# Gated slot attention with a post-norm FFN on one core: ScalarE's copies of the gated transposes and the softmax's exponential change places, and some first transfers and weight sums are reordered

## The chip, the core and the metric

The kernel runs on one core of a Trainium2 chip. The metric is device time in microseconds. The engines are named as in the profile: PE is TensorE's matrix multiply, PEld its weight load, DVE is VectorE, ACT is ScalarE, POOL is GpSimd, SP is SyncE, which issues all transfers here.

## What is computed

The reference is a layer in two halves, each with a residual and a layer norm. The input `x` is 2 x 2048 x 512, all in float32. The heart of the first half, cut:

```python
q, k, v = heads(x @ Wq), heads(x @ Wk), heads(x @ Wv)      # 16 heads; 64, 64, 128
s = clip(heads(x @ Ws), -32, 32)                            # 64 slots
z = cumlogsumexp(s, time); g = exp(z_before - z); p = exp(s - z)
hk = hk * g + k (x) p ; ok = q . hk                         # per time step
pv = softmax(ok)                                            # over the 64 slots
hv = hv * g + p (x) v ; ov = pv . hv
o = rmsnorm(ov) * g_norm_weight * silu(x @ Wg)
x = layernorm(x + o @ Wo)
hidden = fwht(silu(x @ W1.T) * (x @ W3.T))                  # Walsh-Hadamard, 2048 wide
out = layernorm(x + hidden @ W2.T)
```

## The kernel before, in words

**Two phases.** The attention phase makes 64 steps: four groups of four heads (`g`), and for each group 16 chunks of 128 tokens (`n`), both batches side by side. It takes about the first 2430 us of the span. The FFN phase follows; the change does not touch it.

**Products in seven parts.** Every large product is a two by two block product with seven multiplications instead of eight (the Winograd form). So a step has products `q` (queries, keys and slot logits at once, L503), `v` (values and gates, L529) and `o` (the output projection, L746), each in seven parts 1 to 7, run in the order 1, 2, 5, 6, 7, 3, 4. The parts of one product are summed in three PSUM banks: parts 1, 6, 7, 4 in `c1` (two buffers), 5 and 3 in `c2`, 2 in `c3` (one buffer each; table `SUM`). After a part, VectorE or ScalarE reads the bank (`into`, L458 to L463, for `q` and `v`; L742 for `o`, which adds it to `rows`). `q`, `v` and `o` share the banks. So q2 needs `c3` free, that is, L742 must have read o2 from it; and o3 adds to the `c2` that L742 must have read for o5. Operands need block sums as well: for weights, `Weights.sums` (L408 to L414, four sums `k` = 0 to 3); for the left operand of `o`, `right_factor` (L425): ScalarE copies eight transposes from PSUM (L427, L428), VectorE makes two sums (L432, L433), GpSimd two more (L434, L435), the second from the first. The same `right_sums` serve the input tiles `xb` in the first group.

**Stages.** `run` (called with four steps: `new`, `now`, `before`, `old`) writes out by hand the order in which each engine gets its instructions; each engine's queue keeps that order. In one call step `now` does its `q` and `v` products, its scores and its softmax, while step `before`, one chunk earlier, gets its values, its gating, its transposes (`o_transposed`, L724) and o1, o5, o2; o3, o6, o7, o4 come in the next call, where the step is `old`. Only SP's order is made by the scheduler, from the same program.

**The place of the change in a step.** Part v7 is followed by `softmax` (VectorE: L625 product, L631 maximum, L633 difference; ScalarE: L634 exponential, in place on `r`), then v3, then `softmax_sum` (VectorE L638 sum and L639 reciprocal; GpSimd L640, `r` times `iz`), then `o_transposed` for step `before` (eight transposes L730 on TensorE into PSUM, then `right_factor` into `ob`), then `softmax_end` (VectorE L644, `r` times the reciprocal sum, after L640), then v4, tanh (L539), o1, o5, the gate product L543 and o2. The next call starts with q1, o3 and q2, with now and then a Hadamard product (L854) between o3 and q2, or transposes of finished rows (L905, L921) between o2 and q1. `r` is used next in that call, after q6 (L649).

**The start.** SP issues the input of step 0 (`load_x`: blocks 0 and 1 at L477, block 2 at L478, `b12` at L481), then four blocks of `wqks`, the fourth into the scratch tile `low` (L403), then the input of step 1, `wvg`, `wo_`. In the first step alone the four sums of `wvg` are in the list `late`: sum 0 before v1, sum 2 before v6, sum 1 before v5, sum 3 after v2. v6 needs sum 2, v7 needs sum 1, v3 needs sum 3. One tile `low` serves all weights, so `wo_`'s block into it waits for `wvg`'s sums.

Of the kernel before, what the change touches and what calls it, by code (L numbers as in the profile page):

```python
# [10 lines left out]
AF = mybir.ActivationFunctionType  # L11
# [8 lines left out]
DK = 64  # L20
# [18 lines left out]
def gated_slot_attention_ffn_kernel(  # L39
# [13 lines left out]
    nc = tc.nc  # L53
# [67 lines left out]
    wp = ctx.enter_context(tc.tile_pool(name="wp", bufs=1))  # L121
# [23 lines left out]
    def sums(pool, width, name):  # L145
        return {c: pool.tile([P, width], F32, name=name + c, tag=c, bufs=2 if c == "c1" else 1) for c in ("c1", "c2", "c3")}
# [3 lines left out]
    def open_x(name, outer, width):  # L150

        t = wp.tile([P, 7, 2, width], F32, name=name).rearrange("p a b c -> p (a b c)")
        for i, m in enumerate(outer):
            xb[RIGHT[m]] = t[:, i * 7 * TQ : (i + 1) * 7 * TQ].rearrange("p (k t) -> p k t", t=TQ)
            load_x(0, RIGHT[m])

    def open_acc(names, **where):
        t = where.pop("pool", hp).tile([P, len(names), 4, 2 * TQ], F32, name="acc" + names, bufs=1, **where)
        for i, n in enumerate(names):
            acc[n] = t[:, i]  # L160

    def load_x(blk, at):
        nc.sync.dma_start(out=xb[at], in_=fxd[blk][:, at])
# [46 lines left out]
    def up(u, h):  # L210
# [9 lines left out]
        for i, m in enumerate(OUTER):  # L220
# [13 lines left out]
            for k in INNER:  # L234
                s = c[SUM[k]]
                for j in range(2):
                    nc.tensor.matmul(  # L237
                        s[:, j * TQ : (j + 1) * TQ], lhsT=w[:, LEFT[k], j, :], rhs=right[:, RIGHT[k], :],
                        start=(k in (1, 2, 5) and j == 0), stop=True, skip_group_check=True,
                    )  # L240
                b = BLOCK[k]
                if k in (1, 5, 6, 4):
                    if first is None:
                        nc.scalar.copy(t[to][:, b], s)
                    else:
                        add(t[to], s, b, t[first])
                else:
                    add(t[to], s, b)
                if m in (6, 7) and k in ENDS:
                    o = t["w" if m == 6 else "v"][:, b]  # L250

                    (nc.gpsimd if u or m == 6 else nc.vector).tensor_tensor(o, o, t["u"][:, b], ALU.add)  # L252
                if k == 4:
                    if p == NSET - 1 and blk + 1 < NBLK:
                        load_x(blk + 1, RIGHT[m])
                    if m in (2, 6, 7, 4):
                        at, src = {2: (11, "x"), 6: (12, "w"), 7: (22, "v"), 4: (21, "u")}[m]
                        silu(h, at, t[src])
                yield
# [92 lines left out]
    with ExitStack() as att:  # L352
# [42 lines left out]
        class Weights:  # L395


            def __init__(self, name, blocks, pool=wp):
                width = blocks.shape[-1]
                self.t = pool.tile([P, 7, 2, width], F32, name=name)  # L400
                self.low = c1.tile([P, 2, width], F32, name="low", tag="low")
                for k, dst in enumerate((self.t[:, 0], self.t[:, 1], self.t[:, 2], self.low)):
                    nc.sync.dma_start(out=dst, in_=blocks[k])  # L403

            def sums(self, k, eng=nc.vector):
                t, low = self.t, self.low
# [6 lines left out]
                else:  # L413
                    eng.tensor_tensor(t[:, 6], t[:, 1], t[:, 4], ALU.subtract)  # L414

        def load_qks(g):
            return Weights("wqks", wqks[g])

        def load_vg(g):
            return Weights("wvg", wvg[g])  # L420

        def load_o(g):
            return Weights("wo_", wo[g], wpo)
# [41 lines left out]
        class Step:  # L465
# [4 lines left out]
            def load_x(self):  # L470
                self.xb = xp.tile([P, 7, 2, P], F32, name="xb")
                if self.g:
                    nc.sync.dma_start(out=self.xb, in_=xd[self.n])
                    return

                src = xt[self.n]
                nc.sync.dma_start(out=self.xb[:, 0:2].rearrange("p s c t -> p (s c) t"), in_=src[:, 0:KC])  # L477
                nc.sync.dma_start(out=self.xb[:, 2], in_=src[:, KC + 2 :])  # L478
                t = yp.tile([P, D], F32, name="b12", tag="rows")
                self.b12 = t[:, 0 : 2 * P].rearrange("p (c t) -> p c t", t=P)  # L480
                nc.sync.dma_start(out=self.b12, in_=src[:, KC : KC + 2])  # L481
# [140 lines left out]
            def softmax(self):  # L622

                self.r = r = c1.tile([P, NQ, 2 * M], F32, name="r", tag="r")
                nc.vector.tensor_tensor(  # L625
                    r.rearrange("p q (j m) -> p j q m", j=2), pn,
                    self.iz.rearrange("p q (j m) -> p j q m", j=2), ALU.mult,
                )
                self.r8 = r.rearrange("p q (j m) -> p (q j) m", j=2)
                mx = small.tile([P, 2 * NQ], F32, name="mx", bufs=2)  # L630
                nc.vector.tensor_reduce(mx, self.r8, AX.X, ALU.max)  # L631
                mxb = mx.rearrange("p (h o) -> p h o", o=1).to_broadcast([P, 2 * NQ, M])
                nc.vector.tensor_tensor(self.r8, self.r8, mxb, ALU.subtract)  # L633
                nc.scalar.activation(r, r, AF.Exp, scale=DK**-0.5)  # L634

            def softmax_sum(self):
                self.sm = small.tile([P, 2 * NQ], F32, name="sm")
                nc.vector.tensor_reduce(self.sm, self.r8, AX.X, ALU.add)  # L638
                nc.vector.reciprocal(self.sm, self.sm)  # L639
                nc.gpsimd.tensor_tensor(self.r, self.r, self.iz, ALU.mult)  # L640
# [354 lines left out]
        steps = [Step(g, n) for g in range(NG) for n in range(NCB)]  # L995
        w, nw = {}, {}

        def run(new, now, before, old):


            def do(step, name, *args):
                if step is not None:
                    getattr(step, name)(*args)

            def main(name, k):

                if now is not None:
                    getattr(now, name)(k)
                elif before is not None:
                    for _ in range(FILL[name, k]):  # L1010
                        next(ups)

            def work_on(place):

                if not changes:
                    y["place"] = place
                    next(pieces[0], None)
# [5 lines left out]
            def more():  # L1023

                if old is not None and old.g == NG - 1 and old.n >= NCB - 4:
                    work_on(1)
# [3 lines left out]
            g = now.g if now is not None else NG  # L1030
# [5 lines left out]
            late = [nw["vg"].sums] if now is steps[0] else []  # L1036
# [29 lines left out]
            if last:  # L1066
                nw["qks"] = load_qks(g + 1)
# [20 lines left out]
            do(before, "scores2")  # L1088
            do(now, "within1")
            do(before, "within2")  # L1090
            do(now, "share_of_keys")
            do(before, "share_of_values")
            do(now, "e_transposed")
# [9 lines left out]
            do(before, "gated")  # L1103

            for f in late:
                f(2)
            main("v", 6)
            more()
            for f in late:
                f(1)  # L1110
            main("v", 5)
            if o_last:
                scale_o()
            do(now, "reciprocal", 1)
            main("v", 2)
            more()
            for f in late:
                f(3)

            if last:  # L1120
                nw["qks"].sums(0, nc.gpsimd)
# [5 lines left out]
            do(now, "softmax")  # L1127
            main("v", 3)
            more()
            do(now, "softmax_sum")  # L1130
            if o_last:
                nw["o"].sums(2)
                nw["o"].sums(3, nc.gpsimd)
            do(before, "o_transposed")
            do(now, "softmax_end")
            main("v", 4)
            if last:
# [24 lines left out]
        with tc.manual_schedule(  # L1162
            engines={mybir.EngineType.PE, mybir.EngineType.DVE, mybir.EngineType.Activation, mybir.EngineType.Pool}
        ):
            steps[0].load_x()
            nw["qks"] = load_qks(0)
            steps[1].load_x()
            nw["vg"] = load_vg(0)
            nw["o"] = load_o(0)
            steps[0].make_x()  # L1170
            for k in range(4):
                nw["qks"].sums(k)
            N = len(steps)
            for i in range(N + 2):
                if i == N:
                    open_x("wvg", OUTER[3:], 4 * P)
                    open_acc("ux", tag="h1")
                    ups = up(0, h)
                run(*(steps[j] if 0 <= j < N else None for j in (i + 1, i, i - 1, i - 2)))
            for _ in pieces[0]:  # L1180
                pass
# [110 lines left out]
```

## Time and profile before

| | us |
|---|---|
| median of 3 runs | 3518.95 (3515.03 to 3519.06) |
| the profiled execution's own time | 3517.86 |
| its span, first to last instruction | 3516.1 |
| TensorE busy | 3456.7 |
| first matmul starts | 9.57 |
| length of an ordinary step in the first group | 36.74 |

The profile is of one execution, and its durations are that execution's. A row of a group gives line, engine, operation, tiles (out<-in, buffer numbers left out, so that `t` is `t1` or `t2`, `c` any of the banks), shapes and count, then busy time and the mean of one in ns, then the idle time of the engine before it and what ended that. A row of the timeline gives start, duration, engine, line, operation, tiles, shapes, count, and in brackets the idle time before it and its releaser. A matmul in float32 shows as two passes, so one part of `o` is a row of 4 matmuls. Ends of matmuls are modelled, and spans on GpSimd are rough. The weight loads (PEld) run ahead of the matmuls, so a wait often shows at the load first.

TensorE's granted clock is 1.00 in nearly the whole span.

### The profile page before, as it was taken

The page shows a single profiled execution, that of the slowest core. Times are in us where ns is not written, and L with a number is a line of the kernel's source. Part 1 is how long each engine was busy: PE and PEld are TensorE (multiplying, and loading weights), DVE is VectorE, ACT ScalarE, POOL GpSimd, SP SyncE. Part 2 cuts the span into 40 slices and gives each one's busy share as a digit, 9 for nine tenths or more (in the row PEclk, how much of TensorE's full clock was granted, in tenths as well). Part 3 has the DMA queues.
Part 4 walks back from the last instruction along what each step waited for, and adds up shares of the span by engine and source line. Part 5 has one row for each costly group of instructions (what it writes and reads, how often), then busy time and mean ns, then how long its engine had stood idle before and what let it go on. Part 6 is the DMA issues. An engine that isn't in the chain of part 4 may idle for free. (4 is left out here: it accounts for less than half of the span.)

```text
span 3516.1 us, 75258 instructions
## 1 busy us (share of the span) xinstructions
PE 3456.7 (98%) x31840; PEld 2702.8 (77%) x31840; DVE 2354.9 (67%) x3940; ACT 957.0 (27%) x1712; POOL 1144.2 (33%) x1069
## 2 busy tenths in 40 slices
PE   8999999999999999999999999998999999999998
PEld 6777777677777677677777777776888888888887
DVE  5777776665666765656766677777666756756756
ACT  3333333333333333333333333332111111111110
POOL 1222223221221331221332222223634643643544
PEclk9999999999999999999999999999999999999999
DMA  5334334221122232122222243347555544445431
GB/s 184 118 113 138 118 119 152 93 72 62 55 66 70 94 96 65 52 66 70 74 99 68 69 140 129 102 160 270 171 179 205 174 161 176 156 151 184 163 135 68
DMA packets 208833, 425.03 MB, mean 121 GB/s; under 512 B 19696, under 2 KB 120432, under 8 KB 207472
## 3 DMA queue, kind: packets, MB, share of 16 engines
q1 hardware_dynamic: 208496, 420.22, 35.7%
q8 instruction: 250, 4.10, 0.5%
q14 instruction: 87, 0.71, 0.1%
HBM read 297.47 MB, written 125.30 MB: 120 GB/s over the span
## 5 line engine op out<-in xcount | busy, mean ns | idle before, releaser
L529 PE MATMUL c<-wvg,xb 128*128 128x512 f32 x1792 | 812.7, 598 | 4.0 <-DVE wvg L412 2.0
L529 PEld LDWEIGHTS c<-wvg,xb 128*128 128x128 f32 x1792 | 322.1, 190 | 369.6 <-issue 291.9
L503 PE MATMUL c<-xb,wqks 128*128 128x128 f32 x3584 | 553.2, 277 | 15.7 <-DMA wqks<-wqks_blocks 9.6
L503 PEld LDWEIGHTS c<-xb,wqks 128*128 128x128 f32 x3584 | 479.9, 193 | 43.7 <-DVE rows L742 21.5
L218 DVE TENSOR_TENSOR accux<-c,accux 128x512 f32<-128x512 f32 x496 | 341.4, 691 | 180.9 <-PE c L237 163.5
L276 PE MATMUL dc<-w2t,hid 128*128 128x256 f32 x1792 | 455.3, 379 | 2.1 <-DVE res L283 2.1
L237 PE MATMUL c<-wvg,xb 128*128 128x256 f32 x1792 | 432.0, 380 | 6.1 <-DVE accux L218 5.3
L742 DVE TENSOR_TENSOR rows<-c,rows 128x256 f32<-128x256 f32 x448 | 181.7, 418 | 335.9 <-PE c L746 331.4
L237 PEld LDWEIGHTS c<-wvg,xb 128*128 128x128 f32 x1792 | 338.8, 190 | 56.9 <-DVE accux L218 9.1
L276 PEld LDWEIGHTS dc<-w2t,hid 128*128 128x128 f32 x1792 | 340.2, 190 | 49.5 <-DVE res L283 3.3
L503 PE MATMUL c<-wqks,xb 128*128 128x128 f32 x1792 | 347.4, 276 | 0.0
L463 DVE TENSOR_TENSOR t<-c,kept 128x384 f32<-128x384 f32 (+1 forms) x384 | 230.6, 611 | 155.6 <-PE c L503 147.5
L237 PE MATMUL c<-wqks,xb 128*128 128x256 f32 x1344 | 325.1, 380 | 5.2 <-DVE accux L218 2.3
L458 ACT COPY kept<-c 128x384 f32<-128x384 f32 (+1 forms) x384 | 203.5, 530 | 457.8 <-PE c L503 369.5
L516 POOL TENSOR_TENSOR e<-e,zc 1x512 f32<-1x512 f32 x60 | 76.4, 1273 | 710.0 <-ACT e L515 710.0
L237 PEld LDWEIGHTS c<-wqks,xb 128*128 128x128 f32 x1344 | 253.9, 190 | 44.0 <-DVE accux L218 5.0
L503 PEld LDWEIGHTS c<-wqks,xb 128*128 128x128 f32 x1792 | 273.0, 193 | 0.0
L283 DVE TENSOR_TENSOR res<-dc,res 128x256 f32<-128x256 f32 x448 | 189.2, 423 | 117.9 <-PE dc L276 107.3
L573 DVE RECIPROCAL iz<-z 128x256 f32<-128x256 f32 x128 | 223.9, 1749 | 44.6 <-ACT z L564 44.6
L710 POOL TENSOR_SCALAR ss<-ss 128x8 f32<-128x8 f32 x64 | 12.7, 198 | 685.3 <-DVE ss L708 685.3
L706 DVE TENSOR_TENSOR t<-po,t 64x512 f32<-64x512 f32 (+1 forms) x192 | 131.6, 685 | 95.6 <-ACT sq L704 94.3
L252 POOL TENSOR_TENSOR accw<-accw,accux 128x512 f32<-128x512 f32 x64 | 80.8, 1276 | 275.7 <-DVE accux L218 274.3
(189 smaller groups left out, 4975.7 us busy)
## 6 DMA issues: line engine op xcount, KB each, us to landing
xb<-w13s SPq DMA_DIRECT2D x112, 896.0 KB
xb<-xd SPq DMA_DIRECT2D x48, 896.0 KB
yd<-rows SPq DMA_DIRECT2D x128, 256.0 KB
w2t<-w2s SPq DMA_DIRECT2D x32, 896.0 KB
rows<-yd SPq DMA_DIRECT2D x100, 256.0 KB
xd<-xb SPq DMA_DIRECT2D x16, 896.0 KB
wvg<-fxd SPq DMA_DIRECT2D x16, 896.0 KB
w13s<-inner SPq DMA_DIRECT2D x96, 128.0 KB
```

The source lines that it names most:

```text
L218: nc.vector.tensor_tensor(into[:, b], s, (into if first is None else first)[:, b], ALU.add)
L237: nc.tensor.matmul(s[:, j * TQ : (j + 1) * TQ], lhsT=w[:, LEFT[k], j, :], rhs=right[:, RIGHT[k], :], start=(k in (1, 2, 5) and j == 0), st ...
L252: (nc.gpsimd if u or m == 6 else nc.vector).tensor_tensor(o, o, t["u"][:, b], ALU.add)
L276: nc.tensor.matmul(s, lhsT=h["hid"][:, i, LEFT[m], k * P : (k + 1) * P], rhs=h["w2"][:, i, RIGHT[m], :], start=(m in (1, 2, 5) and i == 0) ...
L283: nc.vector.tensor_tensor(r, s, r, ALU.add)
L458: nc.scalar.copy(self.kept[k], s)
L463: nc.vector.tensor_tensor(t[:, to], s, self.kept[other], ALU.add)
L503: nc.tensor.matmul(out[:, i * P : (i + 1) * P], lhsT=a, rhs=b, start=(k in OPENS and c == 0 and i == 0), stop=(c == 1), skip_group_check=True,
L529: nc.tensor.matmul(out, lhsT=self.xb[:, RIGHT[k], c, :], rhs=w["vg"].t[:, LEFT[k], c, :], start=(k in OPENS and c == 0), stop=(c == 1), sk ...
L573: nc.vector.reciprocal(self.iz[:, h], self.z[:, h])
L706: nc.vector.tensor_tensor(self.gj[to, j], self.po[j][at], self.gj[to, j], ALU.mult)
L742: nc.vector.tensor_tensor(y_, self.uo.sum(k), y_, ALU.add)
```

## The change

Three edits. First, the exponential L634 moves from `softmax` to the head of `softmax_sum`, and `o_transposed` of step `before` moves ahead of `softmax_sum`. So ScalarE's queue has L427, L428 and then the exponential; VectorE's has L432, L433 and then L638, L639; GpSimd's has L434, L435 and then L640. L644 still follows all of them on VectorE. TensorE's order stays as it was. In the steps that sum `wo_` (one in each of three groups), the sums k = 2, 3 stay behind `softmax_sum`.

Second, in the first step the late sums of `wvg` move up: sum 2 from before v6 to just behind `within2` (on VectorE between L584 and L602), sum 1 from before v5 to before v6, sum 3 from behind v2 to before v5 (ahead of the second half of L573).

Third, the first `load_x` issues only blocks 0 and 1 of `xb`; block 2 and `b12` (`load_rest`) follow behind the second block of `wqks`. SP's order changes with it at a few later places: in the first two steps the block of `wo_` into `low` moves ahead of half of a `zc` transfer and a `b12`, blocks 0 to 2 of step 2's input move ahead of three stores of `w13s`, and the store of `xd` for step 2 ahead of some more of those; near the end of the attention phase three transfers of the finished rows and of the FFN's tiles change places.

```diff
-            def __init__(self, name, blocks, pool=wp):
+            def __init__(self, name, blocks, pool=wp, then=None):
...
                 for k, dst in enumerate((self.t[:, 0], self.t[:, 1], self.t[:, 2], self.low)):
                     nc.sync.dma_start(out=dst, in_=blocks[k])
+                    if k == 1 and then is not None:
+                        then()
...
                 nc.sync.dma_start(out=self.xb[:, 0:2].rearrange("p s c t -> p (s c) t"), in_=src[:, 0:KC])
+                if self.n:
+                    self.load_rest()
+
+            def load_rest(self):
+                src = xt[self.n]
                 nc.sync.dma_start(out=self.xb[:, 2], in_=src[:, KC + 2 :])
...
-                nc.scalar.activation(r, r, AF.Exp, scale=DK**-0.5)
 
             def softmax_sum(self):
+                nc.scalar.activation(self.r, self.r, AF.Exp, scale=DK**-0.5)
                 self.sm = small.tile([P, 2 * NQ], F32, name="sm")
...
             do(before, "within2")
+            for f in late:
+                f(2)
             do(now, "share_of_keys")
...
             for f in late:
-                f(2)
+                f(1)
             main("v", 6)
             more()
             for f in late:
-                f(1)
+                f(3)
             main("v", 5)
...
             main("v", 2)
             more()
-            for f in late:
-                f(3)
...
             main("v", 3)
             more()
+            do(before, "o_transposed")
             do(now, "softmax_sum")
             if o_last:
                 nw["o"].sums(2)
                 nw["o"].sums(3, nc.gpsimd)
-            do(before, "o_transposed")
             do(now, "softmax_end")
...
-            nw["qks"] = load_qks(0)
+            nw["qks"] = load_qks(0, steps[0].load_rest)
```

## The prediction

> **What bounds the kernel now.** I read the page first, then TensorE's waits, then the timelines of one ordinary step and of the two places that the change touches elsewhere.
>
> From the page:
>
> ```profile
> PE 3456.7 (98%) x31840; PEld 2702.8 (77%) x31840; DVE 2354.9 (67%) x3940; ACT 957.0 (27%) x1712; POOL 1144.2 (33%) x1069
> L503 PEld LDWEIGHTS c<-xb,wqks 128*128 128x128 f32 x3584 | 479.9, 193 | 43.7 <-DVE rows L742 21.5
> ```
>
> TensorE bounds it: some 60 us of the 3516.1 are idle, so little can be won, while any new TensorE wait adds in full. The second row names a wait that exists already: weight loads of product q2 wait for L742. The list of who waits for whom (total us, times, longest), TensorE's matmuls, then its weight loads:
>
> ```profile
> PE c L503 <- DMA wqks<-wqks_blocks: 9.6, 1, 9.6
> ...
> PE c L746 <- ACT ob L427: 5.0, 8, 1.3
> ...
> PE c L529 <- DVE wvg L412: 2.0, 1, 2.0
> ```
>
> ```profile
> PEld c L746 <- ACT ob L427: 47.8, 64, 2.1
> ...
> PEld c L503 <- DVE rows L742: 21.5, 43, 1.6
> ```
>
> The first three lines are what the change aims at. The last matters most: in 43 of the 63 steps that hold both a softmax and an output product, q2 (bank c3) starts only when L742 has read product o2 from c3. The ordinary step, whose last transpose ends at 74.07:
>
> ```profile
> 73.65 0.69 DVE L633 TENSOR_TENSOR r<-r,mx 128x512 f32<-128x512 f32 x1
> ...
> 74.44 0.63 ACT L634 ACTIVATE r<-r 128x512 f32<-128x512 f32 x1 [5.82 <-DVE r L633]
> ...
> 74.98 0.57 ACT L427 COPY ob<-ps 128x512 f32<-128x512 f32 x1
> ...
> 75.94 1.28 POOL L640 TENSOR_TENSOR r<-r,iz 128x512 f32<-128x512 f32 x1 [3.01 <-PE c L529]
> ...
> 77.25 1.20 DVE L644 TENSOR_TENSOR r<-r,sm 128x512 f32<-128x512 f32 x1 [0.59 <-POOL r L640]
> 77.98 1.06 POOL L435 TENSOR_TENSOR ob<-ob 128x256 f32<-128x256 f32 x1
> ...
> 79.04 1.21 DVE L543 SCALAR_TENSOR_TENSOR t<-th,t 128x1024 f32<-128x1024 f32 x1
> ...
> 80.17 0.95 DVE L742 TENSOR_TENSOR rows<-c,rows 128x256 f32<-128x256 f32 x2
> 80.63 0.52 PEld L503 LDWEIGHTS c<-xb,wqks 128*128 128x128 f32 x4 [0.38 <-DVE rows L742]
> ```
>
> The chain is L640 on GpSimd, then on VectorE L644, L742 twice (o1, o5; from 78.37), L543, L742 for o2 (done 80.58), then q2's load at 80.63. There is no slack in it: what makes L644's end later makes TensorE later.
>
> **The change: the softmax's place, 63 steps.** Instructions stay the same, and TensorE's order does too. ScalarE has both `ob` copies ahead of the exponential; VectorE has L432, L433 ahead of L638, L639; GpSimd has L434, L435 ahead of L640. All three queues run in order. The last step has no softmax and shows the new order alone; its transposes end at 2431.52:
>
> ```profile
> 2431.60 0.59 ACT L427 COPY ob<-ps 128x512 f32<-128x512 f32 x1 [7.88 <-issue]
> 2432.09 0.38 ACT L428 COPY ob<-ps 128x256 f32<-128x256 f32 x1
> ...
> 2432.50 0.43 DVE L432 TENSOR_TENSOR ob<-ps,ob 128x256 f32<-128x256 f32 x1 [1.69 <-ACT ob L428]
> ...
> 2433.00 0.73 POOL L434 TENSOR_TENSOR ob<-ob 128x256 f32<-128x256 f32 x1 [2.63 <-DVE ob L432]
> ...
> 2433.81 0.72 POOL L435 TENSOR_TENSOR ob<-ob 128x256 f32<-128x256 f32 x1
> ```
>
> Laid on the step at 74.07: L427 at 74.15, L428 to 75.02, exponential (its input is ready at 74.34) 75.0 to 75.6, 0.55 later than now. VectorE: L432 75.05 to 75.47, L433 to 75.8, L638 to 76.41, L639 to 76.65. GpSimd: L434 75.55 to 76.28, L435 76.36 to 77.08. Only then L640, 77.05 to 78.33, though its input was there at 76.65. L644 starts at 78.36 instead of 77.25, 1.11 later.
>
> How long L644 then takes is one choice. It takes 1.20 beside L434 and L435, but 0.69 in the first step, where GpSimd stands idle after L640:
>
> ```profile
> 46.09 0.69 DVE L644 TENSOR_TENSOR r<-r,sm 128x512 f32<-128x512 f32 x1 [1.22 <-POOL r L640]
> ```
>
> In the new order nothing follows L640 on GpSimd, so I take 0.69: L644 ends at 79.05 against 78.45. The other choice is L435: 1.06 in ordinary steps, 0.72 alone. The Trainium skill (SBUF — State Buffer, "Who interferes with whom") says that a VectorE instruction with two SBUF inputs contends with a GpSimd one that reads SBUF, and that one with a single SBUF input, or a reduction, does not. L435 would now lie beside L638 and L639, both of the free kind: by the rule 0.72, shift 0.60; by the row of ordinary steps 1.06, shift 0.94. GpSimd's sum L408 of `wo_` (128x512), beside the reduction L631, takes 1.28 like L640 of the same shape: I take 0.60.
>
> Cost by step. 35 ordinary steps have q2's first matmul within 0.06 of o2's L742: 35 x 0.60 = 21.0. At three group ends GpSimd sums `wqks` until 2.84 after the transposes; L434, L435, L640 in a row then end at 5.65 against 4.08, L644 shrinks by 0.5: 3 x 1.07 = 3.2. In three steps that sum `wo_`, about 0.8 each, 2.4; in the last two softmax steps 0.7 each, 1.4. In twelve steps of the last group TensorE transposes rows (L905) between o2 and q1, and q2 starts 0.79 after L742: free. In eight steps L854 lies between o3 and q2 (0.77): q2 is free, o3 waits for o5's L742 some 0.1: 0.8. Sum 28.8 us. The ScalarE waits that go (5.0 at matmuls, some 0.1 hidden in the other loads) give nothing in the 43 steps: q2's wait is next and grows by what they shrink. `r` itself has time: its transposes (L649) come 8 us after L644. Tanh and v4's copy keep their times, as ScalarE is free from 75.6.
>
> **The change: the start.** The first matmul waits for `wqks` block 0, issued at 3.05 behind three `xb` transfers; two of them now go behind block 1, so it is issued 0.95 earlier, with 262 KB less ahead. q1 would start at 7.5 to 8.6 instead of 9.57. But q5 needs `low`, whose place is unchanged: L408 ended at 13.37, and q5 began at 14.82. So at most 1.4 is won, at least 0; I take 1.2. `wvg`'s issues slip by up to 2 us; its first use is at 22.68 and its sums start at 23.73.
>
> **The change: the first step's weight sums.** L412 now comes before L602 and the reciprocal L573, L414 before the second L573.
>
> ```profile
> 31.57 8.83 PE L529 MATMUL c<-wvg,xb 128*128 128x512 f32 x16 [1.96 <-DVE wvg L412]
> ...
> 32.55:35.97 3.42, 3.42 (x6) 1.36 (x5) 1.76 (x2) 0.59 (x1) 0.00 (x0) 0.50 0.69 184
> ```
>
> L412 takes 1.16 and would end at 27.6; L602 ends 28.0, before ScalarE's settle copy at 28.88 lets L617 go. The 1.96 goes, and 0.29 at v3. The second line is from the busy times by stretch (TensorE, loads, VectorE, ScalarE, GpSimd, then the granted clock): 0.50 granted for 3.42 us after a stretch (29.14 to 32.55) with TensorE busy 1.45 of 3.41. The Trainium skill (TensorE: Matmul & The Clock Gate, Part 1) has half clock follow at least one idle window; by its letter that window was not idle, and nothing would be won. By the row the gap brought it: 3.42 x 0.5 = 1.7 won. I side with the row. `low` of `wo_` is issued some 1 us sooner; half of zc, `b12` and the `w13s` stores behind moved entries on SP slip by a few us, each with tens of us to its use. Sum: 1.2 + 1.96 + 0.29 + 1.7 = 5.2 won.
>
> **Sum.** 28.8 - 5.2 = +23.6 on the profiled execution's own 3517.86: 3541.5. That execution lies 1.1 below the median of 3518.95, within the runs' spread; I say 3541.
>
> **Rivals.**
> - Not slower (10%): GpSimd's spans are rough, and L434 with L435 may hold it far less than 1.5 us. It decides once both take under 1.1 (75.55 to 76.65): then L640 starts as soon as L639 ends, L644 ends 0.1 later than now, and the waits for L427 are gone: -5.2 - 5.0 + 43 x 0.1 = 3512. For: loads wait for L427 in all 64 steps, 0.75 each. Against: L434 and L435 stand 0.08 apart at 0.73 and 0.72, and L644 starts 0.03 after L640's end, so that those spans fit their neighbours.
> - Half of it (8%): L742's wait grows by only 0.1 to 0.3 (L432 starts on L427 alone, shorter gaps): about 43 x 0.2 = +9, less 5.2, 3522.
> - Larger (12%): L435 at 1.06, shift 0.94: 35 x 0.94 + 8, and 0.2 in the free steps, less 5.2: 3558; with L644 still at 1.20 beyond that.
> - The start does nothing because the transfers share the engines anyway: 3542, inside the main case.
>
> **Numbers.** Main case 70%: 3530 to 3552. The range, to both sides, 3520 to 3558. A measurement can tell 0.2%, about 7 us, from no change: slower 0.83, same 0.11, faster 0.06.
>
> **What would show it.** Right: L640 ends near 4.3 after the transposes (now 3.15), L644 lasts 0.69, q2's load waits for L742 with more than twice the 21.5 us, L746's waits for L427 nearly vanish, ordinary steps are 37.3 us apart instead of 36.74; no half clock near 32. Wrong: step length unchanged in the first group, or L640 starting before L435 ends.

## The result, and the profile after

The changed kernel takes 3549.91 us (median of 5 runs, 3547.49 to 3555.39) against 3518.71 before: ratio 1.0095, 95% interval 1.0081 to 1.0109, 31 us slower where 22 were forecast. The whole interval lies above 1, so the loss is clear of noise. The profiled execution is the slowest of the five, 3555.39 with a span of 3553.6; sums below are made against its span, 37.5 above that of before (3516.1).

Behind the edited place the changed file counts lines higher: L408 is L410, L427 L429, L428 L430, L432 L434, L434 L436, L435 L437, L503 L510, L529 L536, L543 L550, L634 L643, L638 L645, L639 L646, L640 L647, L644 L651, L742 L749, L746 L753. Rows have the numbers of their own run's file. From the page after:

```profile
PE 3476.5 (98%) x31840; PEld 2727.2 (77%) x31840; DVE 2321.1 (65%) x3940; ACT 959.3 (27%) x1712; POOL 1120.2 (32%) x1069
L510 PEld LDWEIGHTS c<-xb,wqks 128*128 128x128 f32 x3584 | 487.9, 196 | 57.6 <-DVE rows L749 41.3
```

VectorE's busy time fell by 34 and GpSimd's by 24, although they execute the same instructions: in the ordinary step L644 takes 0.69 instead of 1.20, and L435 0.73 instead of 1.06, as they no longer run beside each other. That bought nothing, because the bound is TensorE's wait at q2, which nearly doubled (21.5 to 41.3 at the loads). The list of TensorE's waits, at matmuls and then at loads:

```profile
PE c L510 <- DVE rows L749: 19.7, 41, 3.8
PE c L753 <- DVE rows L749: 12.5, 11, 1.9
...
PE c L510 <- DMA wqks<-wqks_blocks: 6.4, 1, 6.4
```

```profile
PEld c L510 <- DVE rows L749: 41.3, 62, 4.2
...
PEld c L753 <- DVE rows L749: 18.2, 49, 1.6
PEld c L753 <- ACT ob L430: 14.4, 60, 0.2
```

The wait for the first copy (5.0 at matmuls, 47.8 at loads before) is gone; a short one for the second copy is left at the loads. In its place stand L749's, now at q2 in 62 steps instead of 43, and at o3 (L753) too. The same ordinary step as before, whose last transpose now ends at 66.79:

```profile
66.82 0.59 ACT L429 COPY ob<-ps 128x512 f32<-128x512 f32 x1 [5.49 <-PE ps L737]
...
67.57 0.65 ACT L643 ACTIVATE r<-r 128x512 f32<-128x512 f32 x1
67.72 0.42 DVE L434 TENSOR_TENSOR ob<-ps,ob 128x256 f32<-128x256 f32 x1
...
68.22 0.73 POOL L436 TENSOR_TENSOR ob<-ob 128x256 f32<-128x256 f32 x1 [2.58 <-DVE ob L434]
...
68.39 0.68 DVE L645 TENSOR_REDUCE sm<-r 128x8 f32<-128x512 f32 x1
...
69.03 0.73 POOL L437 TENSOR_TENSOR ob<-ob 128x256 f32<-128x256 f32 x1
69.10 0.20 DVE L646 RECIPROCAL sm<-sm 128x8 f32<-128x8 f32 x1
...
69.72 1.27 POOL L647 TENSOR_TENSOR r<-r,iz 128x512 f32<-128x512 f32 x1
...
71.02 0.69 DVE L651 TENSOR_TENSOR r<-r,sm 128x512 f32<-128x512 f32 x1 [1.72 <-POOL r L647]
...
73.42 0.75 DVE L749 TENSOR_TENSOR rows<-c,rows 128x256 f32<-128x256 f32 x2
73.90 0.52 PEld L510 LDWEIGHTS c<-xb,wqks 128*128 128x128 f32 x4 [0.74 <-DVE rows L749]
```

The first copy comes 0.88 sooner against the transposes. But GpSimd reaches L647 only after both its sums, VectorE then idles 1.72 in front of L651 (0.59 before) with the L749s queued behind it, and q2's load waits 0.74 instead of 0.38.

By kind of step, from the ends of the transposes in both traces:

| steps | change, us |
|---|---|
| start, to the first transposes | -7.3 |
| 35 ordinary | +19.7 (0.56 each) |
| 8 with L854 between o3 and q2 | +0.6 |
| 12 with L905 | -0.2 |
| 3 that sum `wqks` | +7.6 |
| 3 that sum `wo_` | +7.8 |
| last 2 with a softmax | +7.3 |
| after the last transposes | +1.9 |

The eight steps of the last three kinds are dearer than the mechanism's price. One of them, busy times by stretch (TensorE, loads, VectorE, ScalarE, GpSimd, then the granted clock, DMA share, GB/s):

```profile
596.00:599.42 3.42, 1.50 (x7) 1.05 (x8) 3.32 (x6) 0.00 (x0) 1.82 (x1) 1.00 1.02 418
599.42:602.83 3.41, 3.41 (x19) 3.41 (x18) 1.06 (x2) 0.00 (x0) 3.22 (x2) 0.50 0.63 263
```

Two waits for L749 (1.37 at o3, which begins before this stretch, and 1.21 at q2) leave TensorE busy 1.50 of 3.42, and in the next 3.41 the clock is granted by half. The profile after has eight such stretches in the eight steps, one of them of double length: with TensorE at work throughout 9 x 3.41 / 2 = 15.4 us, of 22.8. That is an upper estimate, and not all of it is the change's: the profile before has no half clock in the last two of these steps, but three other profiles with the old softmax order have it there (between 2394 and 2427), and in them these two steps are 0.8 to 3.4 us longer than in the profile before.

### The profile page after: what moved, and what is told of

Same layout as the page of the kernel before. It is cut to its first block, busy times and chain, and to the rows that moved or that the text cites. A ratio compares the mean times of both kernels' runs of the same rounds, so it can differ in the third digit from the quotient of the medians.

```text
span 3553.6 us, 75219 instructions
## 1 busy us (share of the span) xinstructions
PE 3476.5 (98%) x31840; PEld 2727.2 (77%) x31840; DVE 2321.1 (65%) x3940; ACT 959.3 (27%) x1712; POOL 1120.2 (32%) x1069
## 5 line engine op out<-in xcount | busy, mean ns | idle before, releaser
L536 PE MATMUL c<-wvg,xb 128*128 128x512 f32 x1792 | 810.7, 597 | 1.7 <-DVE t L465 0.9
L536 PEld LDWEIGHTS c<-wvg,xb 128*128 128x128 f32 x1792 | 321.6, 189 | 365.5 <-issue 289.6
L510 PE MATMUL c<-xb,wqks 128*128 128x128 f32 x3584 | 562.9, 280 | 27.1 <-DVE rows L749 19.7
L510 PEld LDWEIGHTS c<-xb,wqks 128*128 128x128 f32 x3584 | 487.9, 196 | 57.6 <-DVE rows L749 41.3
L749 DVE TENSOR_TENSOR rows<-c,rows 128x256 f32<-128x256 f32 x448 | 178.8, 420 | 330.7 <-PE c L753 330.6
L510 PE MATMUL c<-wqks,xb 128*128 128x128 f32 x1792 | 351.7, 279 | 0.0
L510 PEld LDWEIGHTS c<-wqks,xb 128*128 128x128 f32 x1792 | 277.7, 196 | 0.0
```

Source lines behind the costliest of these rows:

```text
L510: nc.tensor.matmul(out[:, i * P : (i + 1) * P], lhsT=a, rhs=b, start=(k in OPENS and c == 0 and i == 0), stop=(c == 1), skip_group_check=True,
L536: nc.tensor.matmul(out, lhsT=self.xb[:, RIGHT[k], c, :], rhs=w["vg"].t[:, LEFT[k], c, :], start=(k in OPENS and c == 0), stop=(c == 1), sk ...
L749: nc.vector.tensor_tensor(y_, self.uo.sum(k), y_, ALU.add)
```

## The experiments

My theory: L644 (here L651) is late, VectorE's queue carries that to L742 of o2, and bank c3 carries it to q2; three orders add up in it (exponential, VectorE, GpSimd); half clock follows where the waits get long. Rivals: the moved transfers; ScalarE's order alone; GpSimd's order alone. Each run below was timed beside the kernel before, whose median moves by some 3 us from one set of runs to the next, so differences are taken within a set.

**Start only.** The softmax as before, the other two edits kept:

```diff
+                nc.scalar.activation(r, r, AF.Exp, scale=DK**-0.5)
 
             def softmax_sum(self):
-                nc.scalar.activation(self.r, self.r, AF.Exp, scale=DK**-0.5)
...
-            do(before, "o_transposed")
             do(now, "softmax_sum")
...
+            do(before, "o_transposed")
             do(now, "softmax_end")
```

> Only the transfers and the first step's weight sums are reordered; the softmax's place is as before. Chain theory (the loss comes from L644 reaching q2's bank late): the ordinary step stays 36.74 us, the first step's gain of 7.3 us seen in the profile of the changed kernel stands alone: 3511 to 3512, no half clock near 32. If the start's gain were paid back later by the transfers that moved, 3518 to 3520.

Measured: 3510.14 against 3517.88, ratio 0.998 (0.9972 to 0.9987). The ordinary step is 36.74. The start's gain stands; the moved transfers cost nothing later.

**Softmax only.** The opposite: of the change only these lines.

```diff
-                nc.scalar.activation(r, r, AF.Exp, scale=DK**-0.5)
 
             def softmax_sum(self):
+                nc.scalar.activation(self.r, self.r, AF.Exp, scale=DK**-0.5)
...
+            do(before, "o_transposed")
             do(now, "softmax_sum")
...
-            do(before, "o_transposed")
             do(now, "softmax_end")
```

> Only the softmax's place is changed; the start is as before. Chain theory: ordinary step 37.31 us as in the changed kernel, 3550 + 7 = 3557. If part of the loss came from the moved transfers, less: 3545 to 3552.

Measured: 3556.67, ratio 1.0112 (1.0098 to 1.0126), ordinary step 37.30. The two halves add up: -7.7 and +38.8 give +31. The whole loss lies in the softmax's place.

**ScalarE's order only.** `right_factor` is split, so that the copies alone stand ahead of the exponential:

```diff
-                right_factor(self.ob, tp)
+                nc.scalar.copy(self.ob[:, 0:2].rearrange("p s c t -> p (s c) t"), tp[:, 0:4])
+                nc.scalar.copy(self.ob[:, 2], tp[:, 6:8])
+                self.tp12 = tp[:, 4:6]
+            def ob_sums(self, engines):
...
             do(now, "softmax_sum")
...
+            do(before, "ob_sums", "vp")
             do(now, "softmax_end")
```

> The changed kernel, but only ScalarE keeps the new order (both copies ahead of the exponential); VectorE has L638 and L639 ahead of its two ob sums and GpSimd has L640 ahead of its two, as before. Chain theory: the exponential ends at 1.47 after the transposes, L640 at 3.6, L644 3.64 to 4.84 (1.20, stretched again), 0.44 later than before: ordinary step 37.15, about 3518.7 - 7.3 + 43 x 0.4 = 3528. GpSimd's order as sole cause: 3512. ScalarE's order as sole cause: 3550.

Measured: 3533.26, ratio 1.0047 (1.0033 to 1.0061). The ordinary step is 37.17, as expected, and ScalarE's order as the sole cause (3550) falls. In this file L748 is the first of VectorE's two sums, L751 and L752 are GpSimd's, L764 is product `o`. The step whose transposes end at 178.66:

```profile
181.00 1.28 POOL L647 TENSOR_TENSOR r<-r,iz 128x512 f32<-128x512 f32 x1 [3.48 <-DVE sm L645]
181.01 0.39 DVE L748 TENSOR_TENSOR ob<-ps,ob 128x256 f32<-128x256 f32 x1
...
181.45 1.99 PE L764 MATMUL c<-wo__224,ob 128*128 128x256 f32 x8 [0.20 <-DVE ob L748]
...
182.31 1.20 DVE L651 TENSOR_TENSOR r<-r,sm 128x512 f32<-128x512 f32 x1 [0.59 <-POOL r L647]
183.03 1.06 POOL L752 TENSOR_TENSOR ob<-ob 128x256 f32<-128x256 f32 x1
```

L651 starts 3.65 after the transposes and lasts 1.20. So the copies' place costs 0.4 per step here, but by two routes that this run can't tell apart. Product o5 needs L748, which now stands behind L645 and L646, and waits for it, so that q1 starts some 0.4 later too. I had not counted that: the free steps, in which L644's lateness costs nothing, grow by as much (12 steps with L905: +4.8), and the total is 5 above what I expected. No half clock is granted in this execution before its end, and the eight special steps cost nothing (under 0.1 for each kind): there VectorE's L633 ends so late that the exponential starts no later than before, or nearly so.

**GpSimd's sums late.** The changed kernel with VectorE's sums where they are and GpSimd's behind L640: 

```diff
             do(before, "o_transposed")
+            do(before, "ob_sums", "v")
             do(now, "softmax_sum")
...
+            do(before, "ob_sums", "p")
             do(now, "softmax_end")
```

> The changed kernel, but GpSimd's two ob sums stand behind L640; ScalarE and VectorE keep the new order. Chain theory: L640 starts at 2.5 instead of 2.98 and ends at 3.8, but L644 is stretched to 1.20 again by the sums that now run beside it, and ends at 5.0 as in the changed kernel (4.97): ordinary step 37.3. In the three steps that sum wqks, L644 ends some 0.6 earlier, with fewer stretches at half clock: 3536 to 3545. GpSimd's order as sole cause: ordinary step 36.74, 3512.

Measured: 3544.6, ratio 1.0077 (1.0063 to 1.009), ordinary step 37.37. This refutes GpSimd's order as sole cause. In the step that ends its transposes at 179.32:

```profile
181.84 1.27 POOL L647 TENSOR_TENSOR r<-r,iz 128x512 f32<-128x512 f32 x1 [3.67 <-DVE sm L645]
183.08 0.73 POOL L751 TENSOR_TENSOR ob<-ob 128x256 f32<-128x256 f32 x1
183.15 1.20 DVE L651 TENSOR_TENSOR r<-r,sm 128x512 f32<-128x512 f32 x1 [1.21 <-POOL r L647]
```

L651 starts 0.4 sooner than in the changed kernel and takes 1.20 again instead of 0.69, as the sums run beside it. What GpSimd's order costs in waiting it gives back in that duration. The last two runs and the changed kernel differ from one to the next in one order, so the ordinary step can be split by engine: ScalarE's order +0.43 (36.74 to 37.17), VectorE's +0.20 (to 37.37), GpSimd's -0.06 (to 37.31). The total is lower than the changed kernel's because of the steps that sum weights: +4.2 with `wqks` and +1.1 with `wo_` in this profile, against +7.6 and +7.8.

**The eight steps as before.** A flag `keep` (steps that sum `wqks` or `wo_`, and the last two with a softmax) keeps the old order there:

```diff
+            keep = last or o_last or now is not None and now.g == NG - 1 and now.n >= NCB - 2
             do(now, "softmax")
+            if keep:
+                do(now, "softmax_exp")
             main("v", 3)
             more()
-            do(before, "o_transposed")
+            if not keep:
+                do(before, "o_transposed")
+                do(now, "softmax_exp")
             do(now, "softmax_sum")
...
+            if keep:
+                do(before, "o_transposed")
             do(now, "softmax_end")
```

> The changed kernel, but eight steps keep the old order of softmax and copies: the three that sum wqks, the three that sum wo_, and the last two with a softmax. Chain theory: the other steps lose as now (35 x 0.57 + 8 x 0.2), less the start's 7.6: 3518 + 21.6 - 7.6 = 3532, and the half-clock stretches near 600, 680, 1207, 1285, 1821, 1900 and 2395 are gone. If those stretches did not come from the longer waits of these steps, they stay and the time is above 3540.

Measured: 3534.49, ratio 1.0041 (1.0028 to 1.0055). The stretches at half clock near 600, 678, 1207, 1285, 1821, 1900 and 2395 are gone; some remain between 2416 and 2495, at the passage to the FFN. The stretch after the same point of the first group end, as granted here:

```profile
596.00:599.42 3.42, 2.53 (x19) 2.08 (x18) 2.04 (x4) 0.48 (x1) 3.11 (x2) 1.00 1.05 426
599.42:602.83 3.41, 3.41 (x29) 3.26 (x28) 2.96 (x2) 0.96 (x2) 1.93 (x1) 1.00 0.51 214
```

TensorE was busy 2.53 of 3.42, and the full clock stayed. The kernel before, timed beside this one, took 3521.02, so the loss is 13.5 here and 31 in the changed kernel: eight steps out of 63 carry some 18 us of it.

**L644 behind o2.** If the chain is the cause, taking L644 out of it must give all back. The changed kernel with one line moved:

```diff
-            do(now, "softmax_end")
             main("v", 4)
...
             do(before, "o", 2)
+            do(now, "softmax_end")
```

> The changed kernel, with softmax_end (L644 alone) moved behind product o2, so that L742 of o1, o5 and o2 and L543 no longer stand behind it on VectorE; r is next used some 6 us later. Chain theory: q2 starts without a wait, 6.36 after the transposes; ordinary step 36.5, no waits for L742 at q2, no half clock in the attention phase: 3488 to 3500. If the loss came from elsewhere (ScalarE's or GpSimd's order as such), it stays near 3550.

Measured: 3499.58 against 3521.02, ratio 0.9941 (0.9927 to 0.9955). In the step that ends its transposes at 176.24:

```profile
180.06 1.50 DVE L550 SCALAR_TENSOR_TENSOR t<-th,t 128x1024 f32<-128x1024 f32 x1
...
181.49 0.41 DVE L749 TENSOR_TENSOR rows<-c,rows 128x256 f32<-128x256 f32 x1
...
181.82 0.68 DVE L651 TENSOR_TENSOR r<-r,sm 128x512 f32<-128x512 f32 x1
...
182.37 0.63 PEld L510 LDWEIGHTS c<-xb,wqks 128*128 128x128 f32 x4
```

```profile
PEld c L510 <- DVE rows L749: 6.6, 4, 1.7
```

o2 is read by 181.90, and q2's loads follow without a wait; waits for L749 there fall from 41.3 to 6.6 us. Not only the loss is given back: the time lies 21 us under the kernel before. The ordinary step is 36.40. In the attention phase half clock is granted once, at 2407, in the last step.

**The same with the old order.** The start-only kernel, with L644 behind o2:

```diff
             do(before, "o_transposed")
-            do(now, "softmax_end")
             main("v", 4)
...
             do(before, "o", 2)
+            do(now, "softmax_end")
```

> As the one before, but ScalarE, VectorE and GpSimd keep the old order (exponential ahead of the copies): only L644 is moved behind o2, and the start is reordered. Chain theory: no wait for L742 either, but the loads of o1 wait for L427 as before (5.0 us at matmuls and some 0.1 hidden in each step): 3498 to 3506, some 8 us above the one before. If the copies' place is worth nothing, the two are equal.

Measured: 3501.7, ratio 0.9949 (0.9936 to 0.9961), ordinary step 36.51. So the chain was the bound in the kernel before too, and the copies' new place is worth 0.1 per ordinary step once L644 is out of the way. The difference of the two versions is 2 us, not 8: the 5.0 at matmuls lie in the special steps, where one wait gives way to another. At a group end the new order saves 0.70 at o1 but waits 1.27 at q2, against 0.32 here. In the three steps that sum `wo_` it loses 0.9 each: o3 waits 1.56 for GpSimd's sum of the weights, which stands behind its two `ob` sums. By the profiles these six steps cost the new order 2.9, and the other steps win 4.1.

**The better of the two in each step.** `keep` from above, with the line moved:

```diff
             if keep:
                 do(before, "o_transposed")
-            do(now, "softmax_end")
             main("v", 4)
...
             do(before, "o", 2)
+            do(now, "softmax_end")
```

> L644 behind o2 in all steps; the copies ahead of the exponential in the ordinary steps alone, the old order in the eight steps that sum wqks or wo_ or stand at the end. If the new order wins 0.1 in ordinary steps and loses where GpSimd sums weights ahead of it, this takes the better of the two late versions in each step: ordinary step 36.41, 3495 to 3498, some 2 to 4 below the version with the new order in all steps. If those eight steps cost the same in both orders: 3499 to 3500.

Measured: 3496.12 against 3519.16, ratio 0.9938 (0.9924 to 0.9951), the lowest median of all. Against the kernel before it wins 23.0, and the version with the new order everywhere 21.4. The two were not timed beside each other, and their intervals overlap; that it is the better one is not shown.

**The start's two halves**, one profiled execution each, so that their totals decide nothing by themselves. The sums alone, and below the transfers alone (with `then` and `load_rest` of the change):

```diff
             do(before, "within2")
+            for f in late:
+                f(2)
...
-                f(2)
+                f(1)
             main("v", 6)
...
-                f(1)
+                f(3)
             main("v", 5)
```

> The kernel before with only the first step's weight sums moved; softmax and transfers as before. First matmul near 9.6 us, no wait for L412 near 31, no half clock near 32, the transposes of the third call's step end 4.2 us sooner (near 69.9 instead of 74.07): some 3514. If the half clock near 32 comes from elsewhere than the gap, it stays and the gain is 2.3.

```diff
-            nw["qks"] = load_qks(0)
+            nw["qks"] = load_qks(0, steps[0].load_rest)
```

> The kernel before with only the first transfers reordered. First matmul near 6.5 us, the wait for the weight sum and the half clock behind it stay, the transposes of the third call's step end 3.0 us sooner (near 71.0): some 3515.5. If the earlier start were lost again at the block in low, 73.

Measured: 3514.17 for the sums alone and 3515.82 for the transfers alone. The sums alone had neither wait nor half clock near 32. The transfers alone kept the wait:

```profile
29.17 7.13 PE L536 MATMUL c<-wvg,xb 128*128 128x512 f32 x16 [1.95 <-DVE wvg L414]
```

and yet no half clock followed it: transposes at 69.96, not 71.0. The same gap, then, brings half clock in one execution (before, and softmax only) and not in another. The sums' execution began its matmuls at 8.09 with the old transfers, 1.5 sooner than the profile before, so the end of its first transposes, 67.45, tells less than it seems.

## Why the prediction was right, and where it was off

**The mechanism** was right. As medians of the ordinary steps, L640 ends 4.24 after the transposes (4.26 forecast) and L644 4.97 (4.98); L644 takes 0.69, L435 0.73. The exponential came 0.1 sooner than forecast, at 0.83. The two choices of a duration, both for the uncontended value, held. The rule on which L435's rested agrees with the trace, at L434 more than at L435: L434 took 0.73 beside the reduction L638 (68.22 and 68.39 above), while L435 met only the last 0.04 of it and the reciprocal. The step: 37.31 against 37.3 forecast, and 35 x 0.56 = 19.7 against 21.0. That L644 is what reaches q2 is shown by the version that moves it.

**The total** was helped by luck. The softmax half costs 38.8 alone, 10 more than the 28.8 forecast, and the start wins 7.7 instead of 5.2: the second error hides a quarter of the first.

**Free steps**: +0.6 and -0.2 against 0.8 and 0.

**The eight special steps: the term that was mis-sized.** 7.0 was forecast; the profile has 22.8, of which up to 15.4 are half clock, which leaves 7.4 or a little more. In the softmax-only run no half clock fell into the three steps that sum `wqks`, and they cost 2.9 together, against 3.2 forecast: the price of the wait was right, and what it set off was missing. I had used the very row (busy 1.45 of 3.41, then 0.50) for the first step and did not ask where else the change would make such a stretch.

**The start**: 5.2 forecast, 7.3 in the profile, 7.7 by medians. The first matmul starts at 6.43 instead of 9.57, 3.1 sooner where 1.2 were taken; from there to the first transposes 4.1 are won, where 3.95 were forecast for the sums and the clock. The step that failed is that `low`'s "place is unchanged" and so holds q5 back. Its first reader, before and after:

```profile
12.41 0.96 DVE L408 TENSOR_TENSOR wqks<-low,wqks 128x768 f32<-128x768 f32 x1 [5.15 <-DMA low<-wqks_blocks]
```

```profile
10.00 0.96 DVE L410 TENSOR_TENSOR wqks<-low,wqks 128x768 f32<-128x768 f32 x1 [1.13 <-DMA low<-wqks_blocks]
```

It started between 9.95 and 10.65 in all nine profiles with reordered transfers, at 12.41 and 12.64 in two with the old order, and at 10.92 in a third, whose first matmul too came 1.5 sooner. So part of the pair's 2.4 is the execution's, and why the unmoved block lands sooner is open. The clock's 1.7 was won in this pair; that it depends on the execution I had not said.

**The rivals**: not slower fell, as L640 did wait for both sums; the larger case fell with L435 at 0.73. In "what would show it", q2's wait for L742 was to exceed twice 21.5 and reached 41.3; part of it moved to o3.

## What to carry to other kernels

Before an instruction is put ahead of another on one engine, follow the second's consumers through every in-order queue until a PSUM bank or a buffer that the bound engine needs next: here a copy won 0.88 us for a load with little to gain, and delayed a multiply whose result is needed only 7 us later (in the kernel before L644 ends at 78.45, and L649, which reads it, starts at 85.62), but behind which three urgent reads stood. The better move was to take that multiply out of their way. A new wait on TensorE is to be priced with what the clock does after it, in the places where it joins another wait.

## What was not expected of the hardware

Half clock was granted for 3.41 us after stretches of the same length in which TensorE was not idle but busy 1.45 or 1.50 us; at 2.53 it was not. The Trainium skill (TensorE: Matmul & The Clock Gate, Part 1) asks for an idle window; here a half-busy one was followed by the same.

All twelve traces together show more. In each of them the granted clock changes only on a grid of 3.413 us: in the profile after, the stretches from 599.42, 677.92 and 1206.99 lie 23 and 155 such lengths apart. Cut along this grid, from 26 us on, all 36 stretches at full clock with TensorE busy 1.40 us or less were followed by half clock, 9 of 12 with 1.43 to 1.65, and none of some 12,000 with 1.67 or more. So here about half a window's work was the limit. The grid lies elsewhere on the program in each execution, and it decides how much of a wait falls into one window. The gap near 28 us, in the kernel before, in softmax only, and in the transfers alone:

```profile
29.14:32.55 3.41, 1.45 (x19) 0.84 (x16) 3.41 (x3) 0.00 (x0) 0.00 (x0) 1.00 0.12 39
```

```profile
27.57:30.99 3.42, 1.19 (x49) 0.91 (x41) 2.92 (x3) 0.63 (x2) 0.00 (x0) 1.00 0.09 29
```

```profile
27.31:30.72 3.41, 1.55 (x4) 0.83 (x5) 3.41 (x4) 0.00 (x0) 0.00 (x0) 1.00 0.12 39
```

The first two were followed by half clock. The third, at 1.55, was not; it lies in the narrow band where both occur, and the ends of matmuls are modelled, so what decides inside the band stays open.

The changed kernel's five runs reach from 3547.49 at a mean clock of 0.997 to 3555.39 at 0.994. A mean lower by 0.003 over 3550 us is 10.7 us of full clock, enough for the spread of 7.9; that is worked out, not tested.
